# A two-layer decoder in one program: the shared expert of layer 1 moved ahead, half units for small experts, and other dependences at its end

## The chip, the cores and the metric

The kernel runs on one core of one Trainium2 chip. The metric is device time in microseconds. Before the change the median of three runs is 3155.25 us (3146.28 to 3155.63). Each run computes the whole reference once, in float32.

## The reference, cut to what matters

The reference is a pre-norm decoder of two layers over `x` of 32 x 100 rows of 256 values. Each layer is self-attention, cross-attention to a context of 361 rows, and a mixture of experts. Only the end of layer 1 bears on this change: the output of the last cross-attention, its layer norm, and the second mixture of experts:

```python
x = x + _L1_xattn_ref(_layernorm(x), ctx_512, ...)
x = x + _L1_ffn_ref(_layernorm(x), ...)

# inside _L1_ffn_ref: E, K, NG, TG = (64, 8, 8, 4), CAP = 256
scores = sigmoid(x @ gate.T); sfc = scores + e_bias
# the 4 best of 8 groups, then the 8 best experts of each row
xe = zeros((E, CAP, H)).at[sorted_e, pos].set(tok_sorted, mode='drop')
h = silu(einsum('ech,efh->ecf', xe, w1)) * einsum('ech,efh->ecf', xe, w3)
ye = einsum('ecf,ehf->ech', h, w2)
out = segment_sum(where(pos < CAP, ye[...], 0) * w, token)
shared = silu(x @ shared_gate.T) * (x @ shared_up.T) @ shared_down.T
return out + shared
```

An expert keeps at most 256 rows. On these inputs the reference's own routing gives rows to 31 of 64 experts; 23 of them are chosen by more than 128 rows, 18 of these fill all 256 places, and 5615 rows are kept in all. The eight experts with at most 128 rows have 82, 22, 12, 8, 7, 7, 3 and 3.

## The kernel before, in words

The 3200 rows are 25 tiles of 128 (`NF`). Names of buffers matter for reading the profile: `x_sb` holds `x`; `xnT` is the normed `x`, transposed; `x_d` is the DRAM table of 64 + 1 blocks of 256 places into which routed rows are sent; `sum` are two DRAM tables of 3200 x 256 into which the experts' weighted results are added; `we` an expert's weights, `xe` its rows, `ye` its result.

**Cross-attention of layer 1** (`xattn_stream`, L419) walks over 32 batches in four steps each. TensorE's order is written by hand (`manual_schedule`); the other engines' order is made by a scheduler from the program's dependences. When a tile of rows is complete, `between` (L848) runs its output projection (`out_proj`), and after two or three tiles starts a `route` generator (L1533) for them. `tick` (L1687) advances all such generators by one piece at each step, so that routing is spread over the stream. The last piece of a route is one indirect DMA per row tile and choice (eight per tile, L1651), issued by POOL: a **send**. `tick` lets only one send go at a time, and each send depends on the work named `self.after`, so sends are paced by other engines' work.

**`l1_ffn`** (L1707) begins after the last output projection. Ahead of it stand three loads of the shared expert's weights into `wB` (L1719), whose space the cross-attention uses until its last steps. The shared expert is split into `hidden(f, i)` (two products for four tiles, into `ps_s` and `ps_t`, a Silu on ACT, a product on DVE) and `down(f)` (one tile, into `ps_m`, added to `x_sb` by DVE, L1741). Some of these steps (`FIRST1 * 2.6` us of them by the program's own estimate) are placed before the units; between them every ACT and DVE instruction ticks the routes of the last tiles. When all 200 sends are out, POOL sets `flag` (L1764), on which the loads of expert rows wait.

**`list1`** (L1662) counts on the chip which experts have rows and writes their numbers, in ascending order, into `listi`. **`units`** (L1790) then works through 32 places of this list, each a unit of 256 rows: SyncE (SP) reads the expert's number into a register (L1797, L1802), loads weights (L1798, nine ahead, 12 buffers) and rows (L1804, five ahead, 8 buffers). `expert_turn` transposes the rows, `expert_hidden` makes the hidden values one step later, and `expert_add` one step after that makes the result, weights it into `ye` (DVE, L1879, three buffers) and issues two accumulating indirect DMAs of 128 rows each (POOL, L1883): the **scatter-adds**. Unit u adds into table u % 2, and waits until the scatter-adds of unit u - 2, which went to the same table, have landed. What is left of the shared expert is put between the units on TensorE (`beside`, 0.9 us per unit). If more than 32 experts have rows, a branch (`tc.If`) runs 32 more units; here it isn't taken.

At the end SP loads both tables piece by piece (L1784), DVE adds them to `x_sb` (L1786), and ACT's queue stores the output (L1787).

Of the kernel before, what the change touches and what calls it, by code (L numbers as in the profile page):

```python
# [16 lines left out]
P = 128  # L17
NB = 32
# [33 lines left out]
UNITS, MORE = 32, 32  # L52

FIRST1 = 18
# [25 lines left out]
class Kernel:  # L80
# [677 lines left out]

    def load1(self, b):
        self.ctx1[b] = self.cx.tile([CD, LP], F32, tag="cT", name="cT", bufs=3)  # L760
        return self.nc.sync.dma_start(self.ctx1[b], self.a["ctxT"][:, b, :])
# [21 lines left out]
    def l1_xattn(self):  # L783
        nc, tc, a = self.nc, self.tc, self.a
        self.route_begin()
        with ExitStack() as st:
# [7 lines left out]
            class Lay:  # L794
# [52 lines left out]
                def between(s, n, sums):  # L847
# [21 lines left out]
                    if g == 2 and b > 0 and tile_of(b - 1) is not None:  # L869
# [6 lines left out]
                    for _ in range(1 + (n > 4 * NB - 12)):  # L876
                        me.tick(s.after)
                    if 0 <= of < NB:
                        s.rT = me.row_scale(pool, by_row)

# [781 lines left out]
    def list1(self, counts):  # L1662

        nc, rp = self.nc, self.rp
        ps = self.bank_t()[:E1, :2]
        self.mm(ps[:, 0:1], [(counts, self.ones1[:, 0:1])])
        used = rp.tile([E1, 2], F32, tag="used", name="used")
        nc.vector.tensor_single_scalar(used[:, 0:1], ps[:, 0:1], 0.0, op=ALU.is_gt)
        yield 1
        self.mm(ps[:, 1:2], [(self.before1[:E1, :E1], used[:, 0:1])])  # L1670
        nc.vector.tensor_copy(used[:, 1:2], ps[:, 1:2])
        at = rp.tile([E1, E1], F32, tag="at1", name="at1")
        nc.vector.tensor_scalar(at, self.io1[:E1, :], used[:, 1:2], used[:, 0:1], ALU.is_equal, ALU.mult)
        yield 1
        pl = self.bank_t()[:, : E1 + 1]
        self.mm(pl[:, :E1], [(self.row1, at)])
        self.mm(pl[:, E1:], [(self.ones1[:E1, :], used[:, 0:1])])
# [6 lines left out]
        nc.vector.tensor_copy(self.listi[:, 2 * E1 :], pl[:, E1:])  # L1684
# [23 lines left out]
    def l1_ffn(self):  # L1708
        nc, tc, a = self.nc, self.tc, self.a
        x = self.x  # L1710
        with ExitStack() as st:
            self.psum = st.enter_context(self.banks("l1f", s=3, t=3, m=2))
            pool = st.enter_context(tc.tile_pool(name="p1f", bufs=2))
            w = self.wts.tile([P, 3584], F32, tag="wB", name="wB2")
            wg, wu, wd = (
                w[:, o : o + 512].rearrange("p (k n) -> p k n", k=NK) for o in (0, 512, 1024)
            )
            for t, n in ((wg, "sg1"), (wu, "su1"), (wd, "sd1")):
                nc.sync.dma_start(t, a[n].rearrange("(k p) n -> p k n", p=P))  # L1719
            ep = st.enter_context(tc.tile_pool(name="e1f", bufs=2))  # L1720
            sp = st.enter_context(tc.tile_pool(name="s1f", bufs=2))
            hT = {}

            def hidden(f, i):

                n = min(4, NF - f) * P
                if i == 0:
                    hT[f] = sp.tile([P, 2, 4 * P], F32, tag="hT", name="hT")
                h = hT[f]
                pg, pu = self.bank_s()[:, :n], self.bank_t()[:, :n]  # L1730
                for p, ws in ((pg, wg), (pu, wu)):
                    self.mm(p, [(ws[:, k, i * P : (i + 1) * P], self.xn_at(k, f, n // P)) for k in range(NK)])
                g = sp.tile([P, 4 * P], F32, tag="g", name="g")
                self.tick(nc.scalar.activation(g[:, :n], pg, AF.Silu))
                self.tick(nc.vector.tensor_tensor(h[:, i, :n], pu, g[:, :n], ALU.mult))

            def down(f):
                pd = self.bank_m()[:, :D]
                h, at = hT[f // 4 * 4], slice(f % 4 * P, (f % 4 + 1) * P)
                self.mm(pd, [(h[:, i, at], wd[:, i, :]) for i in range(2)])  # L1740
                self.tick(nc.vector.tensor_tensor(x[:, f, :], pd, x[:, f, :], ALU.add))  # L1741

            def shared():

                for f in range(0, NF + 4, 4):
                    for i in range(2):
                        if f < NF:
                            hidden(f, i)
                            yield 3.5
                        for j in range(2):  # L1750
                            if 0 <= f - 4 + 2 * i + j < NF:
                                down(f - 4 + 2 * i + j)
                                yield 0.9

            steps = shared()
            with tc.manual_schedule(engines={mybir.EngineType.PE}):
                us = 0.0
                while us < FIRST1 * 2.6:
                    us += next(steps)
                while self.routes:  # L1760
                    self.tick(self.after)
# [4 lines left out]
            end = self.units(ep, 0, UNITS, steps)  # L1766
            n = nc.values_load(self.listi[0:1, 2 * E1 : 2 * E1 + 1], min_val=0, max_val=E1)
            for u in range(UNITS, E1, MORE):
                with tc.If(n > u):
                    more = self.units(ep, u, u + MORE)  # L1770

                    word = pool.tile([1, 1], F32, tag="word", name="word")
                    got = nc.sync.dma_start(word, self.sum_d[0][0:1, 0:1])
                    self.depend(got, [more.ins], "the units' sums")
# [6 lines left out]
            for f in range(0, NF, 5):  # L1781
                at = slice(f, f + 5)
                for i in range(2):
                    got = nc.sync.dma_start(ends[i][:, at, :], sums[i][:, at, :])  # L1784
                    self.depend(got, [end.ins], "the last sums")
                    nc.vector.tensor_tensor(x[:, at, :], x[:, at, :], ends[i][:, at, :], ALU.add)  # L1786
                nc.scalar.dma_start(out[:, at, :], x[:, at, :])  # L1787


    def units(self, pool, u0, u1, beside=iter(())):  # L1790

        nc, tc = self.nc, self.tc
        we, xes, xTs, hTs, added = {}, {}, {}, {}, {}

# [210 lines left out]
```

## Time and profile before

| what | us |
|---|---|
| median of three runs | 3155.25 |
| profiled execution, as timed | 3155.59 |
| its span in the profile | 3153.6 |
| TensorE busy over the span | 3013.7 (96%) |
| VectorE, ScalarE, GpSimd busy | 1811.1, 1406.8, 926.3 |
| end of the last output projection (TensorE) | 2914.3 |
| shared expert ahead of the units (TensorE) | 2914.9 to 2966.4 |
| first transpose of an expert's rows | 2971.9 |
| first scatter-add issued | 2985.5 |
| last scatter-add's issue ends | 3117.45 |
| final loads, sums and stores | 3121.6 to 3153.6 |

Times inside the span count from its start. In a row of a timeline stand start, duration, engine, line, operation, tiles (out<-in), sizes, the number of instructions merged into the row, and in brackets the idle time of the engine before it and what seems to have ended it. A wait for several things is put down to the one that came last by this profile; where the named engine had long been done, it was another, often a DMA. `SPq` is SP issuing a transfer. The rows themselves are shown with the prediction.

### The profile page before, as it was taken

The numbers are of one execution on the slowest core, as the hardware profiler recorded it, in microseconds if no ns is written. First come the engines' busy times: TensorE is split into PE (matmuls) and PEld (weight loads), VectorE is DVE, ScalarE is ACT, GpSimd is POOL, SyncE is SP. The second block draws the span as 40 slices with busy tenths as digits, with TensorE's granted clock in tenths as the row PEclk, the third lists the DMA queues.
The fourth block names the chain that finished last, engine by engine and source line by source line (L and its number), as shares of the span: only waits on it lengthen the run. The fifth ranks groups of instructions, "written<-read, shape, count | busy, mean of one in ns | idle before, by whom it ended". The sixth has DMA issues, their size and how long they took to land. (4 is left out here: it accounts for less than half of the span.)

```text
span 3153.6 us, 67966 instructions
## 1 busy us (share of the span) xinstructions
PE 3013.7 (96%) x26832; PEld 2261.1 (72%) x26832; DVE 1811.1 (57%) x4686; ACT 1406.8 (45%) x4361; POOL 926.3 (29%) x1048
## 2 busy tenths in 40 slices
PE   8999999999999899999998999999999999998983
PEld 7777777677777658888875677777777777776572
DVE  6666666577777622222227876656666666665443
ACT  5555554566666511222232234545545555454220
POOL 3222221465555451000016420021211212122474
PEclk9999999999999999999998999999999999999996
DMA  8850000000000033554541000010000000000387
GB/s 311 305 197 1 1 1 1 18 14 14 14 14 14 16 129 132 202 192 179 201 153 55 14 5 6 8 41 24 15 11 11 11 11 10 9 10 15 109 204 183
DMA packets 130105, 225.86 MB, mean 72 GB/s; under 512 B 40525, under 2 KB 108421, under 8 KB 122992
## 3 DMA queue, kind: packets, MB, share of 16 engines
q1 hardware_dynamic: 98704, 127.32, 12.6%
q0 software_dynamic: 27792, 90.81, 8.8%
q8 instruction: 215, 3.52, 0.5%
q10 hardware_dynamic: 3280, 3.28, 0.3%
q14 instruction: 114, 0.93, 0.1%
HBM read 153.77 MB, written 113.61 MB: 85 GB/s over the span
## 5 line engine op out<-in xcount | busy, mean ns | idle before, releaser
L1651 POOL DMA_INDIRECT x_d<-xr,slot x200 | 194.5, 972 | 775.3 <-DVE kT L131 243.7
L444 ACT ACTIVATE wBx<-ps_t,m 100x361 f32<-100x361 f32 x512 | 280.8, 560 | 259.7 <-DVE m L441 234.2
L136 PE MATMUL ps_t<-xnT,wA 128*128 128x200 f32 x1536 | 300.6, 340 | 1.9 <-DMA wA<-in_wq 1.3
L136 PEld LDWEIGHTS ps_t<-xnT,wA 128*128 128x128 f32 x1536 | 260.0, 192 | 37.4 <-issue 19.5
L441 DVE TENSOR_REDUCE m<-ps_t 100x1 f32<-100x361 f32 x512 | 241.2, 526 | 79.3 <-PE ps_t L136 77.2
L136 PE MATMUL ps_t<-xT,w 128*128 128x256 f32 x1276 | 283.2, 381 | 0.7 <-ACT xT L130 0.7
L136 PEld LDWEIGHTS ps_t<-xT,w 128*128 128x128 f32 x1276 | 240.0, 190 | 41.7 <-issue 9.3
L614 DVE TENSOR_REDUCE m<-ps_t 100x1 f32<-100x361 f32 x512 | 235.5, 517 | 18.1 <-PE ps_t L136 18.0
L338 POOL TENSOR_TENSOR e<-e,rz 100x400 f32<-100x400 f32 x128 | 109.5, 856 | 407.1 <-DVE rz L337 397.6
L635 ACT ACTIVATE e<-ps_t 121x300 f32<-121x300 f32 x512 | 173.9, 426 | 123.5 <-PE ps_t L136 123.4
L334 ACT ACTIVATE e<-s,m 100x100 f32<-100x100 f32 x512 | 186.1, 365 | 20.8 <-DVE m L328 20.1
L136 PE MATMUL ps_t<-wA,zT 128*128 128x256 f32 x800 | 188.0, 388 | 3.8 <-DVE zT L883 3.0
L136 PE MATMUL ps_t<-kT,qT 64*100 64x361 f32 x1024 | 190.1, 488 | 0.9 <-ACT wBx L444 0.9
L639 POOL TENSOR_TENSOR es<-e 121x400 f32<-121x400 f32 x128 | 132.4, 1034 | 197.0 <-ACT e L635 196.8
L136 PE MATMUL ps_t<-cT,wA 128*128 128x361 f32 x512 | 188.5, 492 | 1.5 <-SPq L1250 1.5
L453 PEld LDWEIGHTS ps_t<-ident,wBx 100*121 100x121 f32 x1536 | 178.1, 186 | 12.7 <-issue 5.7
L136 PE MATMUL ps_t<-wA,cT 128*121 128x512 f32 x384 | 184.9, 593 | 0.6 <-ACT wBx L444 0.6
L453 PE MATMUL ps_t<-ident,wBx 100*121 100x100 f32 x1536 | 185.3, 270 | 0.0
L136 PEld LDWEIGHTS ps_t<-wA,zT 128*128 128x128 f32 x800 | 152.1, 193 | 33.3 <-issue 4.7
L1332 DVE TENSOR_TENSOR h<-ps_t,g 128x256 f32<-128x256 f32 x145 | 61.2, 425 | 199.4 <-ACT g L1331 199.4
L131 DVE COPY eT<-ps_t 121x300 f32<-121x300 f32 x339 | 146.7, 461 | 30.6 <-PE ps_t L453 26.4
L471 PE MATMUL ps_z<-eT,v 121*64 121x100 f32 x3072 | 161.0, 254 | 0.3 <-issue 0.3
(301 smaller groups left out, 5810.6 us busy)
## 6 DMA issues: line engine op xcount, KB each, us to landing
x_d<-fill SPq DMA_DIRECT2D x16, 1284.0 KB
we<-in_wexp SPq DMA_DIRECT2D x32, 384.0 KB
cT<-in_ctxT SPq DMA_DIRECT2D x64, 181.5 KB
xe<-x_d SPq DMA_DIRECT2D x32, 321.0 KB
xe_d<-zero SPq DMA_DIRECT2D x8, 1024.0 KB
xe<-xe_d SPq DMA_DIRECT2D x29, 256.0 KB
y_d<-y SPq DMA_DIRECT2D x29, 256.0 KB
sum<-fill SPq DMA_DIRECT2D x10, 640.0 KB
```

The costliest lines, as they stand in the source:

```text
L131: return self.nc.vector.tensor_copy(out, in_)
L136: self.nc.tensor.matmul(out, lhsT=l, rhs=r, start=(i == 0), stop=(i == n - 1))
L334: nc.scalar.activation(t[:, i, :], s[:, i, :], AF.Exp, bias=m[:, i : i + 1], accum_out=rz[:, i : i + 1])
L338: nc.gpsimd.tensor_tensor(t[:, h, :], t[:, h, :], self.last(rz[:, h], T), ALU.mult)
L441: lay.after = nc.vector.tensor_reduce(m, ps[i], AX.X, ALU.max, negate=True)
L444: nc.scalar.activation(t[:, :L], ps[i], AF.Exp, bias=m, accum_out=sums[b][:, h : h + 1])
L453: nc.tensor.transpose(pt[:, c, :], e[n, i][:, c * KC : (c + 1) * KC], self.ident[:T, :T])
L471: nc.tensor.matmul(out, lhsT=v, rhs=eT[n, i][:, c, :], start=first, stop=last)
L614: nc.vector.tensor_reduce(m[:, j, o : o + 1], ps[r], AX.X, ALU.max, negate=True)
L635: nc.scalar.activation(t[:, r], ps[r].rearrange("p (c t) -> p c t", c=NKC), AF.Exp)
L639: nc.gpsimd.tensor_tensor(s, t[:, :, 0, :], t[:, :, 1, :], ALU.add)
L1651: got = nc.gpsimd.indirect_dma_start(out=self.x1_d[:, :], out_offset=bass.IndirectOffsetOnAxis(ap=slot[:, j, k : k + 1], axis=0), in_=xr[: ...
```

## The change: what it does

Six edits, all at the end of layer 1:

- The shared expert's three weights are loaded with the other weights of layer 1's cross-attention, into a free part of `wA` (`load_late`), not into `wB` at the end. The shared expert becomes a generator, `shared1`, whose first four steps (two `hidden`, two `down`) are placed into the last steps of the cross-attention and into the last output projection. Its buffers are a `qT` tile and later `wB`.
- The last two tiles' route is driven by `last_tile` directly; before it, all earlier routes are drained. `list1` and the rest of the route are interleaved with shared steps at fixed places at the head of `l1_ffn`. All 16 last sends are emitted at once and depend on no later work. `FIRST1` is now 25.0 us of shared steps after these.
- `list1` orders the list: experts with more than 128 rows first, the others after them. The first 24 places are whole units, the next 8 are half units: only 128 rows are loaded, transposed, computed and added (one scatter-add). The branch's number is the larger of (experts with rows - 32) and (experts over 128 rows - 24); its body is the eight second halves and 32 whole units.
- `ye` has five buffers instead of three.
- Shared steps between units start with the fourth unit, 1.0 us per unit.
- The final loads no longer depend on the scatter-adds inside the branch.

```diff
-UNITS, MORE = 32, 32
-FIRST1 = 18
+WHOLE, HALF = 24, 8
+UNITS = WHOLE + HALF
+FIRST1 = 25.0
...
+        ws = self.w1s = [w[:, 6144 + i * 512 : 6656 + i * 512].rearrange("p (k n) -> p k n", k=NK) for i in range(3)]
+        for t, n in zip(ws, ("sg1", "su1", "sd1")):
+            self.load_late(t, a[n].rearrange("(k p) n -> p k n", p=P))
...
+                    if b == NB and g < 2:
+                        if g == 0:
+                            me.shared = me.shared1(pool.tile([P, 8, 2 * T], F32, tag="qT", name="qT"))
+                        next(me.shared)
+                    if b == NB and g == 2:
+                        s.last_tile()
...
+                def last_tile(s):
+                    f, shared = NF - 1, me.shared
+                    zT, po = me.zTs.pop(f), me.bank_m()[:, :D]
+                    for c in range(8):
+                        if c == 4:
+                            next(shared)
+                            next(shared)
+                        nc.tensor.matmul(po, lhsT=zT[:, c, :], rhs=wo[:, c, :], start=c == 0, stop=c == 7)
+                    nc.vector.tensor_tensor(me.x[:, f, :], po, me.x[:, f, :], ALU.add)
+                    me.norm_stats(f, ROUTED)
+                    while me.routes:
+                        me.tick(s.after)
+                    me.after = s.after
+                    r = me.last_route = me.route(NF - 2, 2)
+                    next(r)
+                    next(shared)
+                    next(shared)
+                    for _ in range(10):
+                        next(r)
...
     def list1(self, counts):
...
+        nc.vector.tensor_single_scalar(used[:, 1:2], ps[:, 0:1], float(P), op=ALU.is_gt)
+        nc.vector.tensor_tensor(used[:, 2:3], used[:, 0:1], used[:, 1:2], ALU.subtract)
...
+        nc.vector.tensor_scalar(left[:, 0:1], pl[:, E1 : E1 + 1], float(-UNITS), 0.0, ALU.add, ALU.max)
+        nc.vector.tensor_scalar(left[:, 1:2], pl[:, E1 + 1 :], float(-WHOLE), None, ALU.add)
+        nc.vector.tensor_tensor(left[:, 0:1], left[:, 0:1], left[:, 1:2], ALU.max)
...
-                us = 0.0
-                while us < FIRST1 * 2.6:
-                    us += next(steps)
-                while self.routes:
-                    self.tick(self.after)
+                next(steps)
+                next(steps)
+                (used, _), = self.routes
+                next(used)
+                next(route)
+                us = next(steps)
+                next(used)
+                next(route)
+                us += next(steps)
+                next(used)
+                for _ in route:
+                    pass
+                while us < FIRST1:
+                    us += next(steps)
...
-            end = self.units(ep, 0, UNITS, steps)
+            units = [(u, whole) for u in range(WHOLE)] + [(u, first) for u in range(WHOLE, UNITS)]
+            end = self.units(ep, units, steps)
...
+                    tc.declare_no_dep(got.ins, group="behind", reason="SyncE has waited in the branch")
...
+                at = self.x1_d.rearrange("(e s p) d -> s e p d", p=P, s=2)[halves[0]][bass.ds(e, 1)]
+                got = nc.sync.dma_start(t[:, 0, :], at.rearrange("o p d -> p (o d)"))
...
-                room = room + 0.9 if u < u1 else 100.0
+                if beside and i > 2:
+                    room = room + 1.0 if i < n_all else 100.0
...
-        y = pool.tile([P, 2, D], F32, tag="ye", name="ye", bufs=3)
+        y = pool.tile([P, 2, D], F32, tag="ye", name="ye", bufs=5)
```

In the built programs the order of instructions on every engine is the same up to layer 1's last cross-attention steps, but for the three added loads. One more thing differs in SP's order: in the program before, SP's register reads of many later units stand between the ninth weight load and the first load of rows; in the changed program the first load of rows follows the ninth weight load directly, and each later read stands before its own load.

## The prediction

> **What bounds the kernel now.** I read the page's slices first (TensorE 96% busy, so ordinarily the bound), then busy time by stage for the end of the span. There the picture changes:
>
> ```profile
> core 0: us, PE busy (x) PEld busy (x) DVE busy (x) ACT busy (x) POOL busy (x), PEclk, DMA share, GB/s
> 2937.00:2952.00 15.00, 15.00 (x47) 8.72 (x46) 4.29 (x12) 1.79 (x3) 7.81 (x8) 1.00 0.75 242
> 2952.00:2968.00 16.00, 14.39 (x43) 7.81 (x42) 4.44 (x9) 1.79 (x3) 7.89 (x9) 1.00 0.02 3
> 2968.00:2985.00 17.00, 13.11 (x53) 10.03 (x54) 5.18 (x13) 3.12 (x6) 0.00 (x0) 0.80 0.68 226
> 2985.00:3004.00 19.00, 19.00 (x90) 15.24 (x90) 10.25 (x27) 5.44 (x11) 15.61 (x10) 1.00 0.63 148
> 3004.00:3036.00 32.00, 32.00 (x174) 28.31 (x173) 19.28 (x49) 9.58 (x20) 24.26 (x16) 1.00 0.86 214
> 3036.00:3084.00 48.00, 39.83 (x196) 33.23 (x195) 21.03 (x57) 10.31 (x22) 31.75 (x21) 0.96 0.81 189
> 3084.00:3100.00 16.00, 15.62 (x79) 12.79 (x77) 8.57 (x24) 4.29 (x10) 13.14 (x9) 1.00 0.71 118
> 3100.00:3120.00 20.00, 1.35 (x5) 0.68 (x4) 3.25 (x8) 0.00 (x0) 14.80 (x11) 0.63 0.47 54
> 3120.00:3154.00 34.00, 0.00 (x0) 0.00 (x0) 14.93 (x10) 0.00 (x0) 0.00 (x0) 0.50 0.86 289
> ```
>
> From 2952 to 2968 the DMA engines do nothing (0.02) and POOL nothing but sends; after 3036 TensorE has gaps; from 3100 only scatter-adds and final transfers are left. So the last 240 us hang on two strings in turn: how soon the rows of the experts can be loaded, and how fast the scatter-adds go. The timeline gives the first string:
>
> ```profile
> 2938.53 0.18 DVE L1646 CAST slot<-none 128x16 int32<-128x16 f32 x1 [0.23 <-DVE none L1645]
> ...
> 2941.67 0.97 POOL L1651 DMA_INDIRECT x_d<-xr,slot  x1 [9.06 <-DVE hT L1735]
> ...
> 2962.94 0.97 POOL L1651 DMA_INDIRECT x_d<-xr,slot  x1 [0.30 <-issue]
> 2965.39 0.09 POOL L1764 MEMSET flag<- 1x1 f32 x1 [1.48 <-PE ps_s L136]
> 2968.99 3.24 SPq L1804 DMA_DIRECT2D xe<-x_d  x6
> 2971.89 1.12 PE L1842 MATMUL ps_t<-ident,xe 128*128 128x128 f32 x4 [5.50 <-DMA xe<-x_d]
> ...
> 2985.47 1.60 POOL L1883 DMA_INDIRECT sum<-ye,xe  x1 [19.99 <-DVE ye L1879]
> ```
>
> The last slots are known at 2938.7, the 16 sends run 2941.67 to 2963.91 (each 0.97 + 0.30, and 3.0 + 2.3 us of waiting for DVE), the flag is up at 2965.48, yet SP issues the first rows only at 2968.99: the chain of waits shows SP reading registers (L1797, L1802) from 2951.6 to 2968.7, the 24 reads that stand before that load. The second string:
>
> ```profile
> 3047.75 0.88 DVE L1879 TENSOR_SCALAR ye<-ps_m,by 128x256 f32<-128x256 f32 x2 [4.29 <-DMA sum<-ye,xe]
> 3047.82 0.37 SPq L1804 DMA_DIRECT2D xe<-x_d  x1
> 3048.45 1.54 POOL L1883 DMA_INDIRECT sum<-ye,xe  x1 [2.74 <-DVE ye L1879]
> ...
> 3115.90 1.55 POOL L1883 DMA_INDIRECT sum<-ye,xe  x1 [0.30 <-issue]
> 3118.72 0.09 POOL L1833 MEMSET flag_u<- 1x1 f32 x1 [1.27 <-DMA sum<-ye,xe]
> 3121.61 0.38 SPq L1784 DMA_DIRECT2D xnT<-sum  x1
> ```
>
> Counting rows, 3047.75 is `ye` of unit 16, which waits for unit 13's landing (three buffers); 3048.45 is the scatter-add of unit 15, whose `ye` was long done (3040.07): it waits for the same landing, unit 13's, by the rule of two tables. So all three rows are released together, and the buffer count isn't what holds POOL. A unit's two scatter-adds cost POOL 3.70 us (2 x 1.55 + 2 x 0.30); units 24 to 31, with no loads left beside them, run at that pace; units 17 to 22, all full and with loads, take 4.43 each (3057.76 to 3084.31).
>
> **Part by part, against the profiled execution's 3155.59** (its span is 3153.6; the median shown is 3155.25, the same within 0.01%).
>
> *Shared steps in the last attention steps.* One `hidden` is 3.44 us of TensorE (`ps_s` and `ps_t`, 1.72 each in the chain), one `down` 0.86. Two and two ahead of the last half projection add 8.6 us. TensorE isn't full there: between 2902 and 2912 the stage view gives 5.9 us busy of 10, and the chain has 8.43 us that belong to no named engine. Walking the new order (TensorE product, Silu, DVE product, then the `eT` copies and `zT` queued behind that DVE product), the last projection ends near 2917 instead of 2914.3: +3. Bounds: -3 (the stall was the three weight loads at 2901 to 2904, now gone) and +9 (stall and products add up). DVE's `zT`, ACT's `rT` and their table loads (1.28 each) wait behind the new instructions; this is in the +3. The three weight loads move to the end of layer 0, where the DMA slices show 3 to 5 tenths busy and nothing waits for them until the end: 0.
>
> *Last route.* From the projection's end to the slots it takes 24.4 us now. In the new order: two `down` (1.7), transposes, copy and gates to the scores +5.5; the DVE chain to `acc` 6.9 now, of which 1.4 are shared products that are no longer between: +11.5; TensorE's count product behind two `hidden`: +12.6; then `sfc` to `slot` 3.1 as now and one more shared product: +16. The sends without pacing: 16 x 1.28 = 20.5; earlier sends (16, drained back to back from about 2897) are through by 2918 and aren't in the way. Flag 1.5 after the last, as now: 2917.3 + 38 = 2955.3, against 2965.4.
>
> *SP.* The list is ready at about +19 (its own extra DVE steps, some ten of 0.15 us, and a product behind one more `hidden`), 2936.6; nine weight loads take 14.6 as now (2936.96 to 2951.5), so SP stands at the first rows at 2951.8 and waits for the flag. One register read instead of 24 is in front: the 3.5 us that SP is late now go. First rows +0.4 and 2.85 to land: **first transpose at 2958.6**, against 2971.9. TensorE, with 37 us of work after the projection (7 `hidden` 24.1, 12 `down` 10.3, small products 2.6), is free at 2954. The later reads stay on SP, 0.56 each: per unit two reads and two issues, about 2 us, under any unit's pace.
>
> *Start of the units.* Now 13.6 us pass from first transpose to first scatter-add, since shared steps lie between. Without them until the fourth unit: three transposes (0.44), two hidden (1.73), one result (0.86), row loads about 1 us apart, `ye` 0.45, POOL 0.25: 7.5. **First scatter-add 2966.1**, against 2985.5.
>
> *Scatter phase.* Now 132.0 (2985.47 to 3117.45) for 64 scatter-adds. Half units take away 8, and TensorE, rows and DVE of 8 halves; the number of rows added stays 5615. But the full experts now stand together, without the seven tiny units between them that gave the DMA engines air. I take 4.43 for 20 whole units, 3.72 for the last four (loads running out), and 2.0 for halves (POOL's 1.85 and some): 88.6 + 14.9 + 16.0 = 119.5. **Five `ye` buffers: 0**, as shown above; if I misread that wait, up to the whole way to POOL's pace (first rival).
>
> Here a rule of the Trainium skill is weighed: "DMA: Bandwidth & Descriptors", section "Anatomy of one DMA — SWDGE (gpsimd) path", fits 2.0 us plus bytes over 436 GB/s per transfer. For 128 KB that is 2.3 us, an estimate; with it, unit u + 2 would never wait (1.85 + 2.3 < 7.4), and the phase would be POOL's 24 x 3.70 + 8 x 1.85 = 103.6. The trace has unit 13's second scatter-add start at 3040.45 and land at 3047.63: 7.2 us. The row decides; the rule gives the first rival. The same page (section "Rules for kernel authors", on accumulating transfers) says to wait for the earlier transfer's semaphore before the same bytes are added to again; that speaks against the five buffers too: the order by table must stay, and does.
>
> *TensorE beneath it:* 24 x 3.03 + 8 x 1.5 + 22 of shared steps = 107 < 119.5, not the bound.
>
> *Tail.* From the last scatter-add's end to the first final load 4.2 us now: 1.3 landing, then 2.8 that SP waits past the flag. Without the branch's dependence about 2: -2. Final transfers, 32.0: unchanged.
>
> Sum: 2966.1 + 119.5 = 3085.6 against 3117.45, -31.9; tail -2.1; **-34: 3121.6, say 3121**.
>
> **Rivals.**
>
> (1) *The buffers were the wait.* For it: `ye` stalls 29.8 us in sum on landings, and DVE, in order, holds everything behind. Against: the count of units above. Phase 103.6, so 16 less: 3105.
>
> (2) *The DMA engines become the bound.* Queue shares over the units give 1.95 us of all 16 engines per unit for weights and rows, and 8.5 ns per added row, 2.17 for a full one: 4.1 per dense unit. At the 0.81 to 0.86 busy share reached now, 4.9 per unit: 24 x 4.9 + 16 = 134, 14.5 more: 3136. Against: 12 weights and 8 row sets are there before the first landing.
>
> (3) *The head start is lost:* the attention's last steps stretch by 9 us, or sends or SP are late by as much: 3130.
>
> (4) *Slower:* the branch runs. It needs more than 24 experts over 128 rows; the reference gives 23 (the smallest of them 131, the next 82). Eight second halves and 32 whole units, at 2.0 and 3.70, would add 134: 3255. From the 25th such expert on it decides; with 23 it is unlikely, but a miscount would do it.
>
> (5) *Nothing happens:* the order of instructions shows the moves, so only an unknown wait could cancel 34 us.
>
> **How the numbers follow.** Forecast 0.50; (1) 0.17, (2) 0.19, (3) 0.10, (4) 0.03, (5) 0.01. The forecast's own bounds (+6/-6 for the start, 4.1 to 4.7 per dense unit) give 3109 to 3134. The range reaches over most of (1) and (2): 3102 to 3139. About 0.3%, 9.5 us, is what a measurement can tell from no change, so faster holds 0.95, same 0.02, slower 0.03.
>
> **What would show it.** First transpose near 2959 and first scatter-add near 2966; SP's first row load right after the flag; POOL's whole units about 4.4 apart, in pairs released by a landing, with `ye` no longer stalled on landings; halves about 2 apart; TensorE done some 20 us before POOL. If POOL runs whole units at 3.7 throughout, (1) holds; if the DMA share stands above 0.9 and landings take over 8 us, (2). An SP row for loads inside the branch would make the whole prediction wrong.

## The result

The changed kernel takes 3139.47 us, median of five runs (3135.45 to 3139.73); the kernel before took 3150.55, median of five (3146.28 to 3155.63). The ratio is 0.9959, 95% interval 0.9944 to 0.9974: faster by 0.4%, about 11 us, where 34 were forecast. The profiled execution of the changed kernel is 3138.55, its span 3136.8. Against the profiled execution of before that is 17 us, but that one lay at the top of its kernel's range.

The stage view of the changed kernel, with the columns of the view shown before the change:

```profile
core 0: us, PE busy (x) PEld busy (x) DVE busy (x) ACT busy (x) POOL busy (x), PEclk, DMA share, GB/s
...
2952.00:2968.00 16.00, 12.02 (x36) 6.36 (x34) 1.54 (x3) 0.87 (x3) 9.91 (x12) 1.00 0.41 110
2968.00:2985.00 17.00, 14.06 (x63) 10.48 (x64) 7.89 (x20) 4.27 (x9) 0.90 (x1) 1.00 0.91 292
...
3004.00:3036.00 32.00, 32.00 (x148) 25.20 (x147) 17.37 (x44) 8.56 (x17) 23.77 (x17) 1.00 0.93 231
3036.00:3084.00 48.00, 44.66 (x247) 38.80 (x246) 25.89 (x73) 12.55 (x31) 36.03 (x24) 0.96 0.95 208
3084.00:3100.00 16.00, 7.48 (x46) 5.70 (x44) 4.93 (x16) 1.71 (x6) 11.28 (x8) 0.91 0.20 36
```

From 2952 to 2968 DVE does 1.5 us of work in 16 and ACT 0.9, though TensorE hands them products; TensorE itself has 4 us of gaps. That wasn't expected. The units start no earlier than before, and then run with TensorE full and the DMA engines at 0.93 to 0.95. The timeline of the changed kernel, rows of several engines in order of time:

```profile
2918.73 0.57 DVE L918 TENSOR_TENSOR zT<-ps_z,rT 128x400 f32<-128x400 f32 x1 [6.20 <-remote]
...
2925.14 0.76 DVE L1837 TENSOR_TENSOR x_sb<-ps_t,x_sb 128x256 f32<-128x256 f32 x2 [5.84 <-PE ps_t L138]
...
2944.28 0.17 DVE L1681 CAST slot<-none 128x16 int32<-128x16 f32 x1 [0.23 <-DVE none L1680]
...
2953.25 18.59 SPq L1864 DMA_DIRECT2D we<-in_wexp  x9
...
2961.83 0.42 DVE L1837 TENSOR_TENSOR x_sb<-ps_m,x_sb 128x256 f32<-128x256 f32 x1 [4.54 <-remote]
...
2963.90 0.97 POOL L1686 DMA_INDIRECT x_d<-xr,slot  x1 [0.31 <-issue]
...
2966.45 0.09 POOL L1784 MEMSET flag<- 1x1 f32 x1 [1.58 <-DMA x_d<-xr,slot]
2967.48 1.08 ACT L1829 ACTIVATE wB<-ps_s 128x512 f32<-128x512 f32 x2 [15.13 <-PE ps_t L138]
2968.11 0.69 DVE L1830 TENSOR_TENSOR wB<-ps_t,wB 128x512 f32<-128x512 f32 x1 [5.85 <-ACT wB L1829]
...
2972.68 6.15 SPq L1872 DMA_DIRECT2D xe<-x_d  x6
...
2976.61 0.66 PE L1914 MATMUL ps_t<-ident,xe 128*128 128x128 f32 x4 [1.13 <-DMA xe<-x_d]
...
2984.10 1.60 POOL L1956 DMA_INDIRECT sum<-ye,xe  x1 [17.56 <-DVE ye L1952]
...
3100.78 1.55 POOL L1956 DMA_INDIRECT sum<-ye,xe  x1 [0.51 <-issue]
...
3103.67 0.39 SPq L1806 DMA_DIRECT2D xnT<-sum  x1
```

Three things are to be seen. The Silu at 2967.48 waits for `ps_s`, which TensorE had finished at 2956.9, and for a DVE product of 2945.9; still it starts 10.6 us late. The two DVE rows with 4.54 and 6.20 us of idle time name no releaser ("remote"), and the products that they wait for were done 5 to 7 us earlier. SP's nine weight loads take 18.59 us, against 13.66 before, and SP reaches the first rows 6 us after the flag is up. All this falls into the two stretches in which POOL issues sends back to back, 2907.88 to 2922.90 and 2944.73 to 2964.87, and DVE and ACT go on 2 to 3 us after the last of each.

SP's part of the chain that ended last (start, duration, engine and line; "issue" is time for which the profile shows no reason) tells what its stall looks like:

```profile
2963.88 0.70 issue
2964.59 0.70 issue
2965.28 0.70 SPq L1863
2965.99 0.72 SPq L1864
2966.71 0.70 issue
2968.15 0.33 SPq L1864
```

During the sends SP goes forward in steps of 0.70 us, in register operations too, for which the profile names no wait. From 2967.4 on, until the first rows, none of its instructions takes more than 0.33 us; ACT's late Silu starts at the same moment, 2967.48.

### The profile page after: what moved, and what is told of

It reads as the page before. It is cut to its first block, busy times and chain, and to the rows that moved or that the text cites. A ratio compares the mean times of both kernels' runs of the same rounds, so it can differ in the third digit from the quotient of the medians.

```text
span 3136.8 us, 67846 instructions
## 1 busy us (share of the span) xinstructions
PE 3002.3 (96%) x26802; PEld 2251.5 (72%) x26802; DVE 1806.7 (58%) x4686; ACT 1403.8 (45%) x4361; POOL 911.1 (29%) x1040
## 5 line engine op out<-in xcount | busy, mean ns | idle before, releaser
L138 PE MATMUL ps_t<-xnT,wA 128*128 128x200 f32 (+1 forms) x1600 | 328.0, 349 | 1.5 <-DMA wA<-in_wq 0.9
L138 PEld LDWEIGHTS ps_t<-xnT,wA 128*128 128x128 f32 x1600 | 271.4, 192 | 50.5 <-issue 32.2
L443 DVE TENSOR_REDUCE m<-ps_t 100x1 f32<-100x361 f32 x512 | 241.0, 525 | 78.4 <-PE ps_t L138 76.3
L637 ACT ACTIVATE e<-ps_t 121x300 f32<-121x300 f32 x512 | 173.9, 426 | 123.0 <-PE ps_t L138 123.0
L138 PE MATMUL ps_t<-wA,zT 128*128 128x256 f32 x784 | 181.5, 385 | 0.0
```

The lines of the kernel that those rows point to most:

```text
L138: self.nc.tensor.matmul(out, lhsT=l, rhs=r, start=(i == 0), stop=(i == n - 1))
L443: lay.after = nc.vector.tensor_reduce(m, ps[i], AX.X, ALU.max, negate=True)
L637: nc.scalar.activation(t[:, r], ps[r].rearrange("p (c t) -> p c t", c=NKC), AF.Exp)
```

## The experiments

The profiles of all runs are read from one event, called **A**: the moment at which the slots of tile 22 are known (the end of the last `slot` row but one). It lies ahead of everything that the change moves, and what runs differ by up to it (A at 2878 to 2910) drops out. In the profile of before A is 2895.8, in that of the changed kernel 2898.2. The runs of one series share a chip, with runs of the kernel before on it; ratios are to these, with a 95% interval.

### Series 1: the sends, and SP's weight loads

`few_last`:

```diff
-            for k in range(TOPK):
+            for k in range(1 if f == NF - 2 else TOPK):
```

> Leaves out 14 of the last 16 sends (all but one choice for the last two tiles), so some rows never reach the experts; everything else stands. Theory S (a run of sends with nothing between them holds up the other engines): between the slots and the first transpose the stalls go: no wait of DVE over 3 us (now 4.54 and 5.85), none of ACT over 8 us (now 15.13), and the nine weight loads take about 13.7 us (now 18.59, the kernel before 13.66). SP then stands at the first rows near 2967 instead of 2972.7, first transpose near 2970.5 instead of 2976.6; time about 6 us under the changed kernel. Theory F (the stalls belong to this place of the program, such as instructions being fetched, not to the sends): the stalls and the 18.6 us stay, first rows at 2972.7, time unchanged within 2 us.

Ratio 0.9934 (0.9919 to 0.9949), 3131.98 us against 3151.49. In its timeline the Silu, the DVE product after it, and the weight loads read:

```profile
2952.45 9.68 SPq L1864 DMA_DIRECT2D we<-in_wexp  x9
2953.63 0.60 ACT L1829 ACTIVATE wB<-ps_s 128x512 f32<-128x512 f32 x1 [6.98 <-PE ps_s L138]
...
2960.57 0.69 DVE L1830 TENSOR_TENSOR wB<-ps_t,wB 128x512 f32<-128x512 f32 x1 [3.08 <-PE ps_t L138]
```

Every stall of this stretch is gone, and DVE's longest wait is the 3.08 us in which TensorE makes the next product. (The stall ahead of the last projection stays: `zT` waits 5.53 us.) So the sends cause the stalls, and even the 13.66 us that before needed for nine weight loads were not SP's own pace. The first rows go out at +63.2 (changed kernel +74.4), 5.6 us sooner than expected. Still the first transpose comes only at +71.7 (expected +72.3), since TensorE is busy with shared products without a gap until then: behind the sends stands TensorE as the next bound of the start.

`pace_last`, `pace_both` and `pace_drained` give the pacing back, to the last 16 sends, to both stretches, or to the drained one alone:

```diff
+    def pace(self, op):
+        if self.paced is not None:
+            self.after = op
+            next(self.paced, None)
...
-            nc.scalar.activation(g[:, :n], pg, AF.Silu)
+            self.pace(nc.scalar.activation(g[:, :n], pg, AF.Silu))
...
-                    while me.routes:
+                    while any(r[1] != SEND for r in me.routes):
                         me.tick(s.after)
...
+                next(route)
+                next(route)
+                self.paced = route
+                while us < FIRST1:
+                    us += next(steps)
+                self.paced = None
                 for _ in route:
                     pass
-                while us < FIRST1:
-                    us += next(steps)
```

The third part stands in `pace_both` and `pace_drained`, the last in `pace_last` and `pace_both`.

> The last 16 sends paced again by the shared steps (each waits for one Silu or DVE product), nothing else. Theory S: the stalls of DVE, ACT and SP during these sends go as they do when the sends are left out; the sends end some 3 to 6 us later (about 2969), SP is ready at about 2967, first transpose about 2973, time 2 to 4 us under the changed kernel. Theory F: stalls and the 18.6 us for nine weight loads stay, and the later flag (about 2971) is paid beside them: time the same or up to 5 us above the changed kernel.

> The last 16 sends and those of tiles 21 and 22 that are drained after the last projection are all paced by shared steps. Theory S: in addition to what pacing the last 16 gives, the last projection's DVE add comes back from 2923.0 to about 2918 to 2920 and the slots from 2944.3 to about 2940: time 5 to 8 us under the changed kernel. Theory F: the projection stays at 2923 and the sends, a few of them pushed behind others, end later: time 3 to 8 us above the changed kernel.

`pace_last`: ratio 0.9971 (0.9961 to 0.9981). The Silus wait for 4.56 to 4.85 us each instead of 15, and nine weight loads take 11.8, but the last send ends at +76.5 instead of +66.6, so the first scatter-add comes at +90.9 instead of +85.9. The stalls went as theory S says; the gain that it hoped for did not come, because the flag then decides. `pace_both`: ratio 0.9955 (0.9936 to 0.9974). The projection is added to `x_sb` at +20.9 instead of +28.0 and the slots are known at +36.4 instead of +46.2, the places the prediction gave them; but the last sends, paced, end at +72.0, and the first scatter-add stays at +86.1: no gain, where 5 to 8 us were expected.

`rows_first` changes SP's order alone:

```diff
-            for i in range(9):
+            for i in range(4):
                 weights(i)
             for i in range(5):
                 rows(i)
+            for i in range(4, 9):
+                weights(i)
```

> SP issues four weight loads, then the rows of five units, then the other five weights. If SP's nine weight loads (18.59 us) are what makes the first rows late, four take about 8.3 us, SP waits at the flag (2966.5) and issues the rows at 2967: first transpose near 2970.5, time 4 to 6 us under the changed kernel. If the shared steps on TensorE, late through the stalls, are what the first transpose would wait for next (they end at 2972.5), first transpose near 2973 and time 2 to 4 us under it. If the weights of units 4 to 8 come too late for their products, the gain is given back within the first eight units: time unchanged.

Ratio 0.9959 (0.9944 to 0.9973). SP issues the rows right behind the flag, at +69.2, and still the first transpose comes later, at +80.4: TensorE, behind by the same stalls, isn't through its shared products earlier. The time is that of the changed kernel, where 2 to 6 us less were expected. None of the three is the one wait; flag, SP and TensorE stand within a few us of each other, and the sends delay all three.

### Series 2: one stretch paced, a shifted program, the buffers

`pace_drained` is `pace_both` without the last part of the diff above.

> Only the sends of tiles 21 and 22 that are drained after the last projection are paced (by shared steps and what is left before the last sends); the last 16 run unpaced as in the changed kernel. Counted from the moment tile 22's slots are known. Theory S (unpaced sends hold the other engines up): last projection added to x at +21 (as with both paced; changed kernel +28), slots at +36.5 (now +46), the last sends start at +41, when the earlier ones are through, and end at +61.5, flag at +63 (now +68); DVE and ACT stall during them as before, SP's nine weight loads take 18 us again, first transpose at +71 to +74 (now +78): time 4 to 7 us under the changed kernel. Rival (pacing only moves the sends, and their sum on GpSimd decides): flag at +68 or later, time within 2 us of the changed kernel.

Ratio 0.9961 (0.9948 to 0.9974). Projection +20.9 and slots +37.9 as expected, flag +62.7 instead of +68.2. Then the last 16 sends stall DVE for 7.73 and 7.24 us and SP's loads take 16.3, and the first transpose, at +77.8, gives all of it back: a miss for theory S's price.

`best1` adds `rows_first` and `FIRST1 = 17.0` to it.

> As the run with the drained sends paced, and SP issues the rows of five units after four weight loads instead of nine, and 6 us less of shared work stand ahead of the units. If flag, SP and TensorE are three bounds close to each other, moving all three gives first transpose near +67 (changed kernel +78, the four changes so far alone +72 to +80) and a time 8 to 11 us under the changed kernel. If the shared steps pushed into the units lengthen the scatter phase, this shows as a phase over 122 us and the gain is smaller by that.

Ratio 0.9949 (0.9935 to 0.9964). First transpose +71.9 (expected +67) and first scatter-add +80.0, phase 122.2. By the ratios that is 3 us under the changed kernel, where 8 to 11 were expected, and the two intervals overlap.

`shift` puts 128 tiny copies each on ACT and DVE at the start of the program:

```diff
...
+        for _ in range(128):
+            nc.scalar.copy(idle[1], idle[0])
+            nc.vector.tensor_copy(idle[2], idle[0])
```

> The changed kernel with 128 tiny instructions each on DVE and ACT at the very start, so that every later instruction stands 128 places further on. If the stalls of ACT (15.13 us idle before the Silu) and DVE (4.54 and 5.85) come from the fetch of a further piece of program at a fixed place in it, they move to other instructions or go: no idle of ACT over 10 us before that Silu. If the run of sends holds the engines up wherever they are, the same three stalls stand at the same instructions within 1 us. Time: some microseconds for the extra instructions at the start, no verdict from it.

Everything stands 11 us later (A 2909.6), and the Silu in question waits as before:

```profile
2971.99 0.42 DVE L1842 TENSOR_TENSOR x_sb<-ps_m,x_sb 128x256 f32<-128x256 f32 x1 [4.57 <-issue]
2978.31 1.09 ACT L1834 ACTIVATE wB<-ps_s 128x512 f32<-128x512 f32 x2 [15.09 <-PE ps_t L143]
```

15.09 and 4.57 against 15.13 and 4.54: the same instructions, though each stands 127 places further on. A stall that belongs to a fixed place of the program, as in the expectation's rival, is ruled out as far as a shift by 127 places can tell. That the sends hold up the fetching of instructions wherever they run is another rival, and the shift doesn't test it. The DMA queue that the profile calls `instruction` speaks against it, but doesn't settle it: from 2950 to 2966 of the changed kernel it has one packet, 0.1% of the engines' time, and in `few_last`, without the stalls, the same. The run was good for one thing more: its phase is 123.0, with the same units as the changed kernel's 118.2, so two profiles can differ by 5 us in it.

`before_bufs4` is the kernel before with `bufs=4` for `ye`.

> The kernel before with four result buffers instead of three (five have no room there). The prediction put the buffers at nothing: the scatter phase (first scatter-add's start to last one's end, 132 us) stays within 1.5 us and the time unchanged, though the products into the buffer no longer wait for landings. If the buffers were the wait (first rival), the dense units fall from 4.4 towards 3.7 us and the time by 8 to 16 us.

Ratio 0.9997 (0.9986 to 1.0009), phase 128.8. The first profile of before had 132.0, the two further ones below 128.3 and 129.5, with three buffers. A fourth buffer is worth nothing, as was forecast for the five.

### Series 3: what sets the pace of the units

`no_shared_units` leaves out the shared steps between the units.

> Leaves out the shared expert's last steps (three hidden products and nine or ten down products), which lie between the units: some 20 us of TensorE work, with its DVE and ACT part. In the changed kernel TensorE is busy 20.00 us of each 20 from the second to the twentieth unit, and the DMA engines stand at 0.81 to 1.03 of their share. If TensorE sets the pace of the whole units there (3.03 us a unit and about 1 of shared work), they fall from 4.2 to 3.7 us, GpSimd's pace, and the phase from first to last scatter-add from 118.2 (123.0 with shifted instructions) to 104 to 110. If the DMA engines or the landings set it, as the prediction had it with 4.43, the phase stays at 118 to 123.

```diff
-            end = self.units(ep, units, steps)
+            end = self.units(ep, units, iter(()))
```

Ratio 0.9939 (0.9924 to 0.9954). Two rows of its stage view, to be laid beside 32.00 of 32 and 0.93 above:

```profile
3025.00:3045.00 20.00, 14.99 (x68) 11.94 (x66) 7.02 (x20) 4.12 (x9) 13.90 (x10) 0.91 0.93 217
3045.00:3065.00 20.00, 16.14 (x74) 13.18 (x75) 8.80 (x25) 4.25 (x9) 13.60 (x10) 0.91 0.90 212
```

TensorE falls from full to three quarters, the DMA share stays at 0.90 to 0.93, and the phase is 121.5: TensorE at 100% wasn't the bound. The queue shares of this stretch (2985 to 3085) are 47.5% for SP's loads and 40.5% for the scatter-adds, 88% of all 16 engines. Whether the DMA engines set the pace, or the landings for which scatter-adds wait, isn't separated by these runs. The interval of its ratio overlaps that of the changed kernel.

`room05` spreads the shared steps otherwise (`0.5 if i < WHOLE else 1.2`).

> The shared steps that are left are spread otherwise: half as much of them beside each whole unit, the rest beside the half units, where TensorE idles (6.5 of 15 us busy). If TensorE sets the pace of the whole units, they take 3.7 to 3.9 us, the half units 2.5 to 3 instead of 2.16, the phase falls by 4 to 8 us and the time as much (to 3132 to 3135). If DMA engines or landings set it, the whole units stay at 4.2 and the halves lengthen: time the same or up to 5 us more.

Ratio 0.9955 (0.9941 to 0.9968), phase 121.3: nothing, which says the same.

`whole32` sets `WHOLE, HALF = 32, 0`.

> The changed kernel with 32 whole units and no halves, all else as it is: 64 scatter-adds instead of 56, and 8 more halves' products. If the halves save what the prediction gives them (3.72 minus 2.0 a unit), the phase is 12 to 14 us longer than 118 to 123 and the time 3151 to 3154, as the kernel before. If landings of the rows that are added set the phase, whose number is the same, it changes by less than 4 us.

Ratio 0.9995 (0.9984 to 1.0005), phase 132.7: the last eight units take 29.3 us instead of 17.3. The half units are worth 12.0 us; without them the change is no faster than the kernel before on this chip.

### Series 4 and 5: better versions, and the chip

`best2` is `best1` with one weight load ahead of the first rows, rows and weights then alternating, `FIRST1 = 12.0` and 1.2 us of shared work a unit.

> As best1, but one weight load stands ahead of the first rows instead of four (rows and weights then alternate), and another 5 us of shared work moves from ahead of the units to between them. The scatter phase was 118 to 123 us in ten runs with 24 whole and 8 half units, wherever it began and whatever TensorE had beside it, so an earlier start should count in full. Counted from the moment tile 22's slots are known: flag at +63 as in best1, first rows right after it (best1 +67.9), first transpose +67 (best1 +71.9, changed kernel +78.4), first scatter-add +74.5 (best1 +80.0, changed kernel +85.9), phase 121: time about 5 us under best1 (3134.6) and 10 under the changed kernel, near 3129. If TensorE does become the bound with 1.2 us of shared work a unit, or the weights come too late, the phase is 125 or more and the time no better than best1.

Ratio 0.9968 (0.9956 to 0.9980): 3116.0 us, against 3127.29 for the kernel before on this chip. Here A is at 2880.5, 15 us sooner than in the profiles before, and nothing stalls. So the next series put all versions on one chip; it fell on one of this kind too.

> The changed kernel once more, on the chip of the others: about 11 us under the kernel before, phase 118 to 123 us, first scatter-add at +85 to +86.

> The first better version once more, on one chip with the changed kernel: first scatter-add at +80, so 4 to 6 us under the changed kernel. If its time under the kernel before (17.8 us) was chance, within 2 us of the changed kernel.

> The second better version once more, on one chip with the changed kernel: first scatter-add at +76, so 8 to 10 us under the changed kernel and about 4 under the first better version. If the earlier start is given back in the scatter phase, within 2 us of the first better version.

`few_both` leaves out, as `few_last` does, the sends of both stretches (`1 if f >= NF - 4`):

> The changed kernel without 14 of the 16 sends of tiles 21 and 22 and 14 of the last 16 (all choices but the first are left out), so rows are missing from the experts. Counted from the moment tile 22's slots are known (in the prediction's sum 2895.8): if unpaced sends are the whole miss, everything stands where the prediction put it: last projection added at +21.5, slots at +37, SP's nine weight loads 10 to 14 us, first transpose +62 to +65 (prediction +62.8, changed kernel +78.4), first scatter-add +70 to +72 (prediction +70.3, changed kernel +85.9), and the time some 14 us under the changed kernel. If a good part of the miss comes from elsewhere (TensorE waiting for the last tile's norm, about 6 us, or the shared products in the last attention steps), the projection stays at +28 or the first transpose at +68 or later.

Kernel before on this chip 3124.53. `after_again` 0.9957 (0.9943 to 0.9971), 3109.93 us; `best1_again` 0.9971 (0.9962 to 0.9980), `best2_again` 0.9972 (0.9963 to 0.9981), 3114.5 to 3114.9; `few_both` 0.9961 (0.9947 to 0.9974). The expectations were wrong: the changed kernel, the very same program, has no stalls here, and leaving the sends out brings it nothing. The timeline of `after_again`:

```profile
2918.54 0.18 DVE L1681 CAST slot<-none 128x16 int32<-128x16 f32 x1 [0.23 <-DVE none L1680]
...
2924.89 9.71 SPq L1864 DMA_DIRECT2D we<-in_wexp  x9
...
2940.82 6.15 SPq L1872 DMA_DIRECT2D xe<-x_d  x6
...
2945.56 1.04 PE L1914 MATMUL ps_t<-ident,xe 128*128 128x128 f32 x8
...
2952.66 1.60 POOL L1956 DMA_INDIRECT sum<-ye,xe  x1 [11.87 <-DVE ye L1952]
```

With A at 2880.9 the slots are known at +37.8, SP issues the rows 0.12 us after the flag (+59.8), and the first scatter-add is at +71.8; `few_both` has it at +70.3. On such a chip the two versions cost 4 to 5 us; on one with stalls `best1` had 3134.6 us, 5 less than the changed kernel in runs of its own, with overlapping intervals of the ratios. No version is shown to beat the changed kernel on both kinds.

`before_again` and `before_third` are the kernel before, for further profiles of it.

> The kernel before once more. If the chip is one on which sends hold nobody up (tile 22's slots known near 2881), the stalls that the first profile showed go too: DVE's and ACT's 8.4 us ahead of the last projection, the slow weight loads and register reads of SP, and counted from that moment the first scatter-add comes at +74 to +80 instead of +89.7, the end at about +242 instead of +257.8: the 34 us of the prediction then held some 16 us of stalls that belong to the chip and not to the order of work. If the kernel before doesn't lose by sends (its are paced), the first scatter-add stays at +88 to +90, and its 16 us lie in a shorter scatter phase. On a chip with the stalls (slots near 2896): +88 to +90, phase 129 to 132, as in the profiles so far.

> The kernel before a third time, for a profile on another chip. On a chip without the stalls (tile 22's slots known near 2881): first scatter-add at +74 to +80 and the end at +242 if the stalls lay ahead of the units; first scatter-add at +88 and a phase near 117 if not. On a chip with them: as the two profiles so far (+89, phase 128 to 132).

The first fell on a chip with stalls (3148.01 us; first scatter-add +89.2, phase 128.3), the second on one without (3125.43 us). The timeline of the second:

```profile
2890.46 0.57 DVE L883 TENSOR_TENSOR zT<-ps_z,rT 128x400 f32<-128x400 f32 x1 [2.46 <-PE ps_z L471]
...
2917.45 9.83 SPq L1798 DMA_DIRECT2D we<-in_wexp  x9
...
2947.53 0.66 PE L1842 MATMUL ps_t<-ident,xe 128*128 128x128 f32 x4 [1.49 <-DMA xe<-x_d]
...
2959.98 1.60 POOL L1883 DMA_INDIRECT sum<-ye,xe  x1 [15.34 <-DVE ye L1879]
```

The 8.52 us that DVE lost ahead of the last projection in the first profile of before are 2.46 here, nine weight loads take 9.83 instead of 13.66, and the first scatter-add is at +77.7 instead of +89.7. The stalls were in the kernel before as well: this is what its expectation gave for the case that they lay ahead of the units (+74 to +80).

## Why the prediction was right and wrong

All in us from A, the prediction's times less 2895.8:

| | predicted | changed, stalls | changed, no stalls | before, first profile (stalls) | before, no stalls |
|---|---|---|---|---|---|
| last projection added to `x_sb` | 22.0 | 28.0 | 20.9 | 19.0 | 12.2 |
| last slots known | 37.5 | 46.2 | 37.8 | 43.0 | 36.1 |
| nine weight loads, from the first register read | 14.6 | 22.1 | 10.6 | 14.5 | 10.7 |
| flag | 59.5 | 68.2 | 59.8 | 69.6 | 62.3 |
| first transpose | 62.8 | 78.4 | 64.7 | 76.1 | 65.3 |
| first scatter-add | 70.3 | 85.9 | 71.8 | 89.7 | 77.7 |
| scatter phase | 119.5 | 118.2 | 121.3 | 132.0 | 129.5 |
| from its end to the first final load | 2.1 | 1.3 | 1.4 | 4.2 | 4.2 |
| final block | 32.0 | 33.1 | 32.9 | 32.0 | 31.9 |

(The projection's 22.0 is the predicted end on TensorE, 2917.3, and the 0.5 us to the end of DVE's add that before shows. The slots' 37.5 is 2917.3 + 16.)

**The step that failed is the price of the sends.** The prediction gave them POOL's time alone: "The sends without pacing: 16 x 1.28 = 20.5; earlier sends (16, drained back to back from about 2897) are through by 2918 and aren't in the way", and for SP "nine weight loads take 14.6 as now". On a chip with stalls the drained sends delay the projection by 6.0 us and the slots by 8.7, and the last 16 stretch the weight loads by 7.5 and starve TensorE; together the first scatter-add is 15.6 later than predicted, of which 14.1 are gone on the chip without stalls. Another 2.5 us lie ahead of A, where single runs differ by as much.

**The same step misread the profile of before.** The 8.43 us of "no named engine" ahead of the last projection were seen, and taken for "the three weight loads at 2901 to 2904, now gone" as the favourable bound. Seven sends stand there back to back (2899.9 to 2908.5): in the three profiles of the kernel on chips with stalls (one with four buffers) DVE's `zT` row shows this wait with 8.52 to 8.64 us, on the chip without 2.46, with the same three weight loads in place. So the 19.4 us by which the start was to come sooner set a new order without stalls against an old one with them. Like against like it is 3.8 us with stalls and 6.0 without. This is the larger part of the missing 23 us.

Two terms of the start were mis-sized by the same step. The shared steps were to move the last projection by +3, with +9 as the bound at which "stall and products add up". They move it by 9.0 us with stalls (19.0 to 28.0) and by 8.7 without (12.2 to 20.9): all their 8.6 us of products are paid. That the place itself came out on the chip without stalls (20.9 against 22.0) is luck, since before's stall stood in its sum. And the 3.5 us by which SP was late at the first rows were put down to its 24 register reads. In `before_third` the same reads take 13.3 us instead of 17.0, and SP waits 3.2 us for the flag: that term belonged to the stalls too.

**The order behind the projection was walked correctly.** Where nobody is held up, the projection (by luck), the slots, the flag, the first transpose and the first scatter-add stand within 2 us of their predicted places, and the 7.5 us from first transpose to first scatter-add are 7.5 and 7.1. Only TensorE was forecast too free (37 us of work after the projection, ready at 2954, +58.2): in `few_both`, without sends, it is busy 38.7 of the 42 us from 2902 to 2944 and reaches the first transpose at +63.2. That bound comes next.

**The scatter phase** was right in size, 118.2 against 119.5; over the ten profiles with 24 whole and 8 half units up to series 3 it is 118 to 123. From before's first profile to the changed kernel's it fell by 13.8 us, but that is in part luck: before's 132.0 was the longest of four (the others 128.3, 128.8 and 129.5). On chips without stalls it fell by 8.2, not 12.5. Half units 12.0 (13.8 forecast); buffers nothing, confirmed; "TensorE beneath it: not the bound", confirmed by taking its work away while it showed 100%. **The tail** gave 2.8 (2.1 forecast). The final block, forecast unchanged, took 1.0 more.

For the two profiles on chips with stalls the sum is -3.8 - 13.8 - 2.8 + 1.1 + 2.5 (A) = -16.8, as between the two spans (3153.6 and 3136.8); for the two on chips without it is -6.0 - 8.2 - 2.8 + 1.0 = -16.0 from A on, and -14.6 in the medians of series 5. Of the rivals, (3), the head start lost as sends and SP are late by as much, came nearest: it had the place and 9 us of the 15.6. Of (2) one sign came, a DMA share above 0.9, but at the pace that the forecast had taken; the other, landings over 8 us, isn't seen: the scatter-adds of `after_again` whose landing is recorded took 2.7 to 7.5. (1) is refuted by `before_bufs4`, and by the phase of 118 to 123 with five buffers.

**Open** is why sends hold the other engines up on some chips and not on others, and by what. Whatever it is, it lets SP and ACT go at one moment, 2967.4 in the changed kernel, 2978.3 in `shift`, 2962.6 in `pace_drained`. Leaving out both runs of sends (`few_both`) was tried only on a chip without stalls; where there are stalls, the second run's part is shown by `few_last`, the first one's by pacing (`pace_drained`). Sends spaced by a wait on POOL itself weren't tried.

## What to carry to other kernels

A wait of a profile that belongs to no named engine is a cost of unknown cause: before a change is credited with removing it, find what runs beside it in each place where it occurs, and put it on both sides of the sum or on neither. A burst that is unpaced may cost its neighbours more than its own engine; look at the others' idle time during it, not only at its end. When one engine stands at 100% and a queue near 0.95, take work away from the engine: that tells whether it is the bound.

## What the runs showed of the hardware that wasn't expected

- A run of 7 to 16 indirect transfers back to back on GpSimd (1.28 us each) can leave DVE and ACT standing for 5 to 11 us with all that they wait for done, and slow SP to steps of 0.70 us. With 14 of 16 left out, the stalls are gone (nine weight loads 9.68 us instead of 18.59).
- It goes with the chip: the same program showed it on one and not on another, and so did the kernel before. The kernel before was 3124.5 to 3127.3 us on the chips without it and 3148.0 to 3152.3 on those with it, twice what the change gains. About 10 us of it lie in the stretch of layer 0's gathers by GpSimd (L1259 of before): between `before_again` and `before_third` the issue times differ by -1.6 us at 1214, by +6.5 at 1705 and by +10.6 at 1754.
- While scatter-adds and loads share the DMA engines, the phase kept its 118 to 123 us wherever it began (+70 to +91) and whatever TensorE had beside it.
